# Turning six of the eight layer norm outputs by VectorE blocks and a DRAM round trip instead of TensorE transposes

## The chip, the cores and the metric

The kernel runs on one core of one Trainium2 chip. The metric is the device time of one execution in microseconds (us), the median of several runs; before the change it is 817.98 us (three runs, 817.22 to 819.26). The engines are named as the profile names them: PE is TensorE (matmuls) and PEld its weight loads, DVE is VectorE, ACT is ScalarE, POOL is GpSimd, SP is SyncE, on whose queue nearly all DMAs are issued.

## What is computed

One transformer block with adaptive layer norm, in float32, on x of 4 batches x 512 tokens x 256 features. Cut to what matters:

```
mod = silu(c) @ wmod                      # per batch: sa, ca, ga, sb, cb, gb
h = layernorm(x) * (1 + ca) + sa
x = x + ga * attention(h)                 # 16 heads of 128, causal
h = layernorm(x) * (1 + cb) + sb
x = x + gb * ffn(h)                       # router, 8 experts (2 chosen), shared, core
```

There are thus eight layer norms: one ahead of the attention and one ahead of the FFN, for each of four batches. Every matmul that follows contracts over the 256 features, so the normed tokens must be turned: from tokens on partitions to features on partitions.

## The kernel before, in words

**Precision.** A float32 matmul is made of three in a faster format (`mm3`, L138 to L142): each operand is kept as a rounded high part and a low part, the rest. The rest is a subtraction (`rest`, L147, L148). So L140, L141 and L142 stand for nearly all matmuls, and L148 for nearly all subtractions.

**The norm.** `normed` (L348) takes statistics and writes `xn`, 128 tokens on partitions, four token tiles t and two feature chunks c. `modulated` (L378) turns it: per chunk four TensorE transposes (L390) into a PSUM tile `ptn` of the tag "pj", which has three buffers and is shared with the projections; then scale and shift (on VectorE L397 for the first chunk, on ScalarE L395 for the second), ScalarE's copy of the high part `hTh` (L401) and VectorE's rest `hTl` (L148). The generator yields after each chunk, so that the second chunk's transposes come later in TensorE's order (`end_norm`).

**The attention.** The main loop (L1028) takes heads in groups of four per batch, and in each step scores one head, projects the next (`project`, L448), mixes an earlier one and projects out a still earlier one. A score tile (`ps`, two PSUM buffers) goes through VectorE's reduction (L488), ScalarE's exponential (L498), VectorE's reciprocal (L502) and GpSimd's scaling (L503). The weights `e` are turned too, but not on TensorE: `turned` (L506) has VectorE turn 32x32 blocks (L512, L518) into `T`, writes `T` to DRAM by four DMAs (L524) that set the blocks in place, and loads the result `aT` by one (L528). `parted` (L531) splits `aT` on ScalarE (L535) and GpSimd (L148), and `mixed` (L540) multiplies it by the values, two to three steps later.

**The FFN.** `all_ffn` (L928) runs the chunks of the experts over one batch after another. It begins while the last heads are still mixed. `route` (L599) makes the gates of a batch by a chain of small VectorE and ScalarE instructions (L621 to L676), and writes them to DRAM; `first` (L780) loads an expert's gates into a tile of the tag "spread" (L788, two buffers). `expert` (L846) adds up on VectorE and GpSimd (L859, L863).

**Order.** Only TensorE's order is the program's; the other engines and the DMA queue are put in order when the kernel is built, by a scheduler that estimates times. [...] The norms stand in it so:
- Attention norms: `norm_batch` of batch b + 1 with the first head of batch b's first group, `modulate` two heads later. The very first is made before the loop.
- FFN norms: `finish` (L1001) puts `norm_batch` one step after the last head of a batch is projected out, and `modulate` two steps after that for batches 0 and 1, three for batch 2, and six for batch 3. `route` follows one step later.

Of the kernel before, what the change touches and what calls it, by code (L numbers as in the profile page):

```python
# [11 lines left out]
F32 = mybir.dt.float32  # L12
F32R = mybir.dt.float32r
AF = mybir.ActivationFunctionType
ALU = mybir.AluOpType
# [3 lines left out]
P = 128  # L19
B, S, D = 4, 512, 256  # L20
H, DH = 16, 128
NT = S // P
DC = D // P
# [61 lines left out]
R = 32  # L85
NB = P // R
# [27 lines left out]
def adaln_attention_moe_kernel(  # L114
# [14 lines left out]
    nc = tc.nc  # L129
    const = ctx.enter_context(tc.tile_pool(name="const", bufs=1))  # L130
    work = ctx.enter_context(tc.tile_pool(name="work", bufs=2))
    small = ctx.enter_context(tc.tile_pool(name="small", bufs=2))
    psum = ctx.enter_context(tc.tile_pool(name="psum", bufs=2, space=PSUM))
    dram = ctx.enter_context(tc.tile_pool(name="dram", bufs=1, space=bass.MemoryType.DRAM))
# [9 lines left out]
    def f32(a: bass.AP) -> bass.AP:  # L144
        return a.bitcast(F32)

    def rest(eng, lo, full, hi):  # L147
        return eng.tensor_tensor(lo, full, f32(hi), ALU.subtract)  # L148
# [150 lines left out]
    modT = const.tile([P, 8, B], F32, tag="modT", name="modT")  # L299
# [48 lines left out]
    def normed(b: int, which: int):  # L348

        st = small.tile([P, NT, 6], F32, tag="st", name=f"st_{b}_{which}")  # L350
        mv = small.tile([P, NT, 2], F32, tag="mv", name=f"mv_{b}_{which}")
        for t in range(NT):
            nc.vector.bn_stats(st[:, t, :], xs[b][:, t, :])
        for t in range(NT):
            nc.vector.bn_aggr(mv[:, t, :], st[:, t, :])
        rstd = small.tile([P, NT], F32, tag="rstd", name=f"rstd_{b}_{which}")
        nc.gpsimd.tensor_scalar(rstd, mv[:, :, 1], LN_EPS, 1.0, ALU.add, ALU.mult)
        nc.gpsimd.tensor_tensor(rstd, rstd, minus_half, ALU.pow)
        xn = work.tile([P, DC, NT, P], F32, tag="xn", name=f"xn_{b}_{which}", bufs=1)
        for t in range(NT):  # L360
            nc.vector.tensor_scalar(
                xn[:, :, t, :],
                xs[b][:, t, :].rearrange("p (c d) -> p c d", c=DC),
                mv[:, t, 0:1],
                rstd[:, t : t + 1],
                ALU.subtract,
                ALU.mult,
            )
        return xn


    recent: dict[str, mybir.Instruction] = {}
# [5 lines left out]
    def modulated(b: int, which: int):  # L378


        xn = xns[b, which]
        hi = const.tile([P, DC, S], F32R, tag=f"hTh{b}", name=f"hTh_{b}_{which}")
        lo = const.tile([P, DC, S], F32R, tag=f"hTl{b}", name=f"hTl_{b}_{which}")
        (h2T if which else hT)[b] = hi, lo
        first = not (b or which)
        whole = []
        for c in range(DC):
            ptr = psum.tile([P, S], F32, tag="pj", name=f"ptn_{b}_{which}_{c}", bufs=3)
            for t in range(NT):
                nc.tensor.transpose(ptr[:, ts(t, P)], xn[:, c, t, :], ident)  # L390
            scale = modT[:, 4 * which + 2 + c, b : b + 1]
            shift = modT[:, 4 * which + c, b : b + 1]

            if c and not first:
                nc.scalar.activation(ptr, ptr, AF.Identity, bias=shift, scale=scale)  # L395
            else:
                nc.vector.tensor_scalar(ptr, ptr, scale, shift, ALU.mult, ALU.add)  # L397
            whole.append(ptr)

            for d in (c,) if not first else range(DC) if c == DC - 1 else ():  # L400
                nc.scalar.copy(hi[:, d, :], whole[d])  # L401
                recent["norm"] = rest(nc.vector, lo[:, d, :], whole[d], hi[:, d, :]).ins
            yield
# [5 lines left out]
    def norm_batch(b: int, which: int):  # L409
        if which and b > 1:  # L410
            with tc.issue_after(recent["hidden"]):
                xns[b, which] = normed(b, which)
            return
        xns[b, which] = normed(b, which)
# [563 lines left out]
    with tc.manual_schedule(engines={mybir.EngineType.DVE, mybir.EngineType.Activation}):  # L978
        for _ in modulated(0, 0):
            pass  # L980
# [9 lines left out]
    def modulate(b: int, which: int):  # L990

        m = modulated(b, which)
        next(m)
        begun_norms.append(m)
# [17 lines left out]
    b, h = order[0]  # L1012
# [15 lines left out]
    for n, (b, h) in enumerate(order):  # L1028
# [30 lines left out]
        e, _, exp, by_sum = next(scores)  # L1059
# [138 lines left out]
```

## Time and profile before

| | |
|---|---|
| median of three runs | 817.98 us |
| profiled execution, its own time | 815.89 us |
| span of the profiled execution | 814.1 us |
| mean granted TensorE clock | 0.989 |
| attention, some norms beside it | to about 640 us |
| FFN | from about 630 us |
| DMA traffic | 124.12 MB, 152 GB/s in the mean |

The span reaches from the first to the last instruction of the program; what lies around it is 815.89 - 814.1 = 1.8 us. Groups of instructions are listed by line, engine, operation and tile names (output<-inputs), with a count, a duration and what ended the idle time before them. A duration is that of one instruction from start to end; matmuls overlap, so the price of one in a full stream is read from the distance of starts. The norms that the change touches have their transposes at 79 and 85 us (attention, batch 2), 119 and 123 (attention, batch 3), 569 and 573 (FFN, batch 0), 608 and 613 (batch 1), 653 and 656 (batch 2) and 701 to 702 us (batch 3).

### The profile page before, as it was taken

What the parts mean: (1) busy time and instruction counts of PE and PEld (TensorE: products, weight loads), DVE (VectorE), ACT (ScalarE), POOL (GpSimd) and SP (SyncE); (2) the same over time, 40 slices, a digit from 0 to 9 for tenths busy, and PEclk for the clock granted to TensorE, in tenths of its full rate; (3) what the DMA queues carried; (4) which work ended last, traced back from release to release, by engine and by line L of the source; (5) the groups of instructions that cost most, each with busy time, mean ns of one, the idle gap of its engine ahead of it and who ended that gap; (6) DMA issues with size and microseconds to landing.
All of it is one profiled execution on the core that took longest, in us unless ns stands there. A gap on an engine that the chain in (4) does not pass through costs nothing.

```text
span 814.1 us, 14111 instructions
## 1 busy us (share of the span) xinstructions
PE 776.6 (95%) x4487; PEld 671.2 (82%) x4487; DVE 596.6 (73%) x1734; ACT 490.1 (60%) x1184; POOL 520.6 (64%) x523
## 2 busy tenths in 40 slices
PE   6898999999999999999999999999998998989997
PEld 5677898999978999998899999999887766767775
DVE  5976888777657777766777677778898587795555
ACT  3575667666656765665666666666656334656663
POOL 4665566896756688675656886656556245565675
PEclk9999999999999999999999999999999899999999
DMA  7376454665775456657555675644576333322221
GB/s 234 102 254 190 130 156 132 183 184 155 219 229 158 135 171 186 179 159 209 160 145 159 174 194 146 186 132 140 153 195 206 105 123 85 101 57 74 57 82 61
DMA packets 73218, 124.12 MB, mean 152 GB/s; under 512 B 8996, under 2 KB 51252, under 8 KB 73144
## 3 DMA queue, kind: packets, MB, share of 16 engines
q1 hardware_dynamic: 73112, 123.21, 52.4%
q8 instruction: 36, 0.59, 0.3%
q14 instruction: 38, 0.31, 0.1%
q0 software_dynamic: 32, 0.02, 0.0%
HBM read 73.05 MB, written 50.14 MB: 151 GB/s over the span
## 4 chain that ended last, share of the span: by engine, by line
PE 72%; DVE 10%; DMA 7%; POOL 4%; ACT 2%; issue 2%; SPq 2%; DVEq 0%; ACTq 0%; POOLq 0%
PE acc L835 4%; PE ps L140 3%; PE pz L140 3%; PE pz L141 3%; PE pz L142 3%; PE ps L141 3%; PE ps L142 3%; PE po L140 3%; PE po L141 3%; PE po L142 3%; PE pk L141 3%; PE pk L140 3%; PE pk L142 3%; PE pv L140 3%; PE pv L142 3%; PE pv L141 3%
## 5 line engine op out<-in xcount | busy, mean ns | idle before, releaser
L148 POOL TENSOR_TENSOR aT<-aT,aTh 128x1152 fp32r<-128x1152 f32 x64 | 172.0, 2687 | 109.0 <-ACT aTh L535 105.9
L503 POOL TENSOR_SCALAR e<-e,inv 128x128 f32<-128x128 f32 (+3 forms) x256 | 135.1, 542 | 68.7 <-DVE inv L502 66.2
L498 ACT ACTIVATE e<-e,nmax 128x128 f32<-128x128 f32 (+3 forms) x256 | 143.3, 561 | 49.7 <-DVE nmax L488 48.9
L535 ACT CAST aTh<-aT 128x1152 fp32r<-128x1152 f32 x64 | 74.0, 1157 | 122.8 <-DMA aT<-moved 61.9
L488 DVE CUSTOM_DVE_ANT_0 e<-ps,mask 128x128 f32<-128x128 f32 (+3 forms) x256 | 120.3, 478 | 28.6 <-PE ps L482 17.8
L518 DVE STREAM_TRANSPOSE T<-e 128x384 f32<-128x384 f32 (+2 forms) x256 | 100.5, 445 | 10.2 <-POOL e L503 10.1
L140 PE MATMUL ps<-kh,ql 128*128 128x256 f32 (+2 forms) x192 | 71.6, 373 | 12.4 <-DVE nmax L488 12.4
L148 DVE TENSOR_TENSOR zl<-pz,zh 128x512 fp32r<-128x512 f32 x64 | 43.9, 687 | 48.9 <-ACT zh L553 48.2
L140 PE MATMUL po<-wo,zl 128*128 128x256 f32 x256 | 73.1, 286 | 1.0 <-DVE zl L148 1.0
L140 PE MATMUL pv<-wv,hTl 128*128 128x256 f32 x256 | 72.0, 281 | 0.5 <-DVE hTl L148 0.5
L141 PE MATMUL po<-wo,zh 128*128 128x256 f32 x256 | 72.1, 282 | 0.0
L142 PE MATMUL po<-wo,zh 128*128 128x256 f32 x256 | 72.0, 281 | 0.0
L141 PE MATMUL pv<-wv,hTh 128*128 128x256 f32 x256 | 71.5, 279 | 0.0
L142 PE MATMUL pv<-wv,hTh 128*128 128x256 f32 x256 | 71.5, 279 | 0.0
L502 DVE RECIPROCAL inv<-tot 128x1 f32<-128x1 f32 x256 | 40.2, 158 | 40.8 <-ACT e L498 33.6
L863 POOL TENSOR_TENSOR oacc<-oacc,part 128x512 f32<-128x512 f32 x28 | 40.9, 1461 | 43.4 <-DVE part L859 36.5
L141 PE MATMUL ps<-kl,qh 128*128 128x256 f32 (+2 forms) x192 | 65.4, 340 | 0.3 <-DVE kl L148 0.3
L140 PE MATMUL pz<-aTh,vl 128*128 128x512 f32 (+2 forms) x192 | 65.0, 339 | 0.0
L141 PE MATMUL pz<-aT,vh 128*128 128x512 f32 (+2 forms) x192 | 64.9, 338 | 0.0
L142 PE MATMUL ps<-kh,qh 128*128 128x256 f32 (+2 forms) x192 | 64.9, 338 | 0.0
L142 PE MATMUL pz<-aTh,vh 128*128 128x512 f32 (+2 forms) x192 | 64.9, 338 | 0.0
L140 PEld LDWEIGHTS ps<-kh,ql 128*128 128x128 f32 x192 | 36.5, 190 | 22.3 <-DVE nmax L488 15.3
(216 smaller groups left out, 2332.1 us busy)
## 6 DMA issues: line engine op xcount, KB each, us to landing
moved<-T SPq DMA_DIRECT2D x256, 160.0 KB, 2.8
aT<-moved SPq DMA_DIRECT2D x64, 640.0 KB, 4.0
spread<-gates_e SPq DMA_DIRECT2D x32, 256.0 KB, 3.3
st_wqk<-in_wqk SPq DMA_DIRECT2D x16, 256.0 KB, 3.7
wf_first<-wfp_first SPq DMA_DIRECT2D x5, 512.0 KB, 4.7
st_wv<-in_wv SPq DMA_DIRECT2D x8, 256.0 KB, 3.3
st_wo<-in_wo SPq DMA_DIRECT2D x8, 256.0 KB, 3.4
wmod<-in_wmod SPq DMA_DIRECT2D x6, 256.0 KB, 5.6
```

The lines of the kernel that those rows point to most:

```text
L140: nc.tensor.matmul(o, lhsT=wl, rhs=mh, start=start, stop=False)
L141: nc.tensor.matmul(o, lhsT=wh, rhs=ml, start=False, stop=False)
L142: nc.tensor.matmul(o, lhsT=wh, rhs=mh, start=False, stop=stop)
L148: return eng.tensor_tensor(lo, full, f32(hi), ALU.subtract)
L488: least = nc.vector.tensor_tensor_reduce(out=et, in0=ps[:, :n], in1=maskf[:, S - n :], scale=-SCALE, scalar=BIG, op0=ALU.add, op1=ALU.min, ...
L498: exp = nc.scalar.activation(et, et, AF.Exp, bias=nm[:, t : t + 1], scale=-1.0, accum_out=tot[:, t : t + 1])
L502: nc.vector.reciprocal(inv[:, one], tot[:, one])
L503: by_sum = nc.gpsimd.tensor_scalar(et, et, inv[:, one], 1.0, ALU.mult, ALU.mult)
L518: nc.vector.transpose(to[:, first : first + n], blocks[:, at : at + (n - 1) * step + 1 : step])
L535: nc.scalar.copy(hi, full)
L835: nc.tensor.matmul(acc, lhsT=w2(k, b), rhs=act[:, s], start=c == 0, stop=c == n - 1)
L863: recent["added"] = nc.gpsimd.tensor_tensor(oacc, oacc, to, ALU.add).ins
```

## The change

The outputs of the first two attention norms are still turned by TensorE (`by_pe`). For the six others, `normed` itself has VectorE turn each chunk in 32x32 blocks into a tile `ntb`, of the tag "spread" for the first chunk and "tmp" for the second; four DMAs a chunk write it to DRAM (`nm`), and one DMA a chunk loads it back with features on partitions, into `hF` (`nhf` in the trace), which takes over the one buffer of the tag "xn". `modulated` then has no TensorE work: ScalarE writes the high part by scale and shift from `hF`, VectorE applies the same scale and shift in place and takes the rest. Both read and write SBUF. All of it, other than TensorE's transposes before, is put in place by the scheduler.

```diff
@@ normed @@
-        return xn
+        return xn if by_pe(b, which) else moved_norm(b, which, xn)
+
+    def by_pe(b: int, which: int) -> bool:
+        return which == 0 and b < 2
+
+    def moved_norm(b: int, which: int, xn):
+        moveds = []
+        for c in range(DC):
+            tag = ("spread", "tmp")[c]
+            tb = work.tile([P, NB, NT * R], F32, tag=tag, name=f"ntb_{b}_{which}_{c}")
+            nc.vector.transpose(
+                tb.rearrange("p i (t r) -> p t i r", r=R),
+                xn[:, c].rearrange("p t (i s) -> p t i s", s=R),
+            )
+            moved = dram.tile([NB, R, NB, NT * R], F32, tag=f"nmoved{c}", name=f"nm_{b}_{which}_{c}")
+            for a in range(NB):
+                nc.sync.dma_start(
+                    moved[:, :, a, :].rearrange("i s x -> s i x"), tb[a * R : (a + 1) * R]
+                )
+            moveds.append(moved)
+        hF = work.tile([P, DC, NB, NT, R], F32, tag="xn", name=f"nhf_{b}_{which}", bufs=1)
+        for c, moved in enumerate(moveds):
+            nc.sync.dma_start(
+                hF[:, c].rearrange("p a t r -> p a (t r)"),
+                moved.rearrange("i s a x -> (i s) a x"),
+            )
+        return hF
@@ modulated @@
         (h2T if which else hT)[b] = hi, lo
+        if not by_pe(b, which):
+            by_block = "p (t a r) -> p a t r"
+            for c in range(DC):
+                full = xn[:, c]
+                scale = modT[:, 4 * which + 2 + c, b : b + 1]
+                shift = modT[:, 4 * which + c, b : b + 1]
+                hi_c, lo_c = (a[:, c, :].rearrange(by_block, a=NB, r=R) for a in (hi, lo))
+                nc.scalar.activation(hi_c, full, AF.Identity, bias=shift, scale=scale)
+                nc.vector.tensor_scalar(full, full, scale, shift, ALU.mult, ALU.add)
+                recent["norm"] = rest(nc.vector, lo_c, full, hi_c).ins
+                yield
+            return
         first = not (b or which)
```

## The prediction, before the changed kernel was run

> **What bounds the kernel now.** I read the page first (busy shares and slices), then the windows, the tile that the change removes, the order of work on TensorE and VectorE where the norms stand, the chain of waits, and the DMA queue.
>
> ```profile
> span 814.1 us, 14111 instructions
> PE 776.6 (95%) x4487; PEld 671.2 (82%) x4487; DVE 596.6 (73%) x1734; ACT 490.1 (60%) x1184; POOL 520.6 (64%) x523
> ```
>
> ```profile
> 130.00:140.00 10.00, 10.00 (x63) 9.07 (x62) 8.07 (x26) 6.63 (x19) 7.37 (x8) 1.00 0.44 125
> ...
> 630.00:640.00 10.00, 8.99 (x37) 7.34 (x37) 9.33 (x31) 3.22 (x6) 3.73 (x3) 0.68 0.32 74
> ...
> 670.00:680.00 10.00, 7.90 (x24) 5.02 (x25) 9.97 (x23) 3.70 (x9) 6.59 (x8) 0.83 0.22 56
> ```
>
> Columns of a window: length, then busy us of PE, PEld, DVE, ACT, POOL, then the granted TensorE clock. From 90 to 590 us TensorE is the bound: no idle time in nearly every window, so a microsecond of its work taken away shortens the span. From 590 to 680 it is not: TensorE idles, VectorE is busy 9.3 to 10 of 10, and after two of the gaps the clock falls (0.68, 0.83). The transposes that go are these:
>
> ```profile
> L390 PE MATMUL ptn<-ident,xn x64: 270/273/477, 10.3 to 702.2; 128*128 128x128 f32 x64
> L401 ACT CAST hTh<-ptn x16: 564/588/607, 12.7 to 704.2; 128x512 fp32r<-128x512 f32 x16
> L148 DVE TENSOR_TENSOR hTl<-ptn,hTh x16: 651/690/692, 13.5 to 704.9; 128x512 fp32r<-128x512 f32 x16
> L397 DVE TENSOR_SCALAR ptn<-ptn,modT x9: 789/817/819, 11.9 to 702.2; 128x512 f32<-128x512 f32 x9
> L395 ACT ACTIVATE ptn<-ptn,modT x7: 750/762/767, 45.6 to 702.5; 128x512 f32<-128x512 f32 x7
> ```
>
> 273 ns is the time of one, not its price, since matmuls overlap. The price is read from starts on TensorE:
>
> ```profile
> 122.77 0.40 PE L142 MATMUL pk<-hTh,wqk 128*128 128x512 f32 x1
> 123.14 0.63 PE L390 MATMUL ptn<-ident,xn 128*128 128x128 f32 x4
> 123.53 0.48 PE L140 MATMUL ps<-kh,ql 128*128 128x512 f32 x1
> 123.84 0.39 PE L141 MATMUL ps<-kl,qh 128*128 128x512 f32 x1
> ```
>
> Undisturbed, starts are 0.23 apart, so L141 would start at 123.23; it starts at 123.84, which makes 0.61 for a group of four. Other groups, by the same sum: 0.45 at 119.25, 0.67 at 85.3, 0.59 at 572.6, and 1.05 for the eight at 701.4. I take 1.07 per norm batch.
>
> [...] The kernel already does this for its attention weights, whose rows price it below. [...] L641 takes 260 ns alone, but
>
> ```profile
> 629.88 2.64 POOL L148 TENSOR_TENSOR aT<-aT,aTh 128x1152 fp32r<-128x1152 f32 x1 [1.65 <-ACT aTh L535]
> ```
>
> ```profile
> 631.18 1.49 DVE L641 TENSOR_TENSOR lt<-lt,r_f 32x128 f32<-32x128 f32 x1
> ```
>
> it ends only after that GpSimd instruction. The change moves hTl's two inputs (one was in PSUM) into SBUF. [...]
>
> **Part by part**, for six of eight batches: attention norms 2 and 3, FFN norms 0 to 3; I call them A2, A3, F0 to F3.
>
> TensorE loses 6 x 1.07 = 6.4 us. A2, A3, F0, F2 and F3 (701 us) lie where it is the bound: -5.3. F1's (608 to 613) stand just ahead of waits on VectorE, so it would only wait longer: 0. No PSUM tile is taken (ptn shares "pj" with projections); that I cost at nothing, from 0 to -0.4 a batch (F2's transposes waited for it some 0.4).
>
> VectorE gains two 128x512 block transposes. The rows for T<-e are 268, 405 and 553 ns for 128, 256 and 384 columns; continued, 0.70 each, 1.40 a batch (bounds 1.1, twice the 0.55 of 384 columns, to 1.5). Both chunks get tensor_scalar on SBUF instead of one in PSUM: L361 took 391 ns at its least for 256 columns, so 0.53 to 0.69 for 512; 2 x 0.66 - 0.82 = +0.5. GpSimd waits: the like instruction al<-hid,ah has a mean of 1016 ns against 671 alone, xn 589 against 391, so 2 x 0.35 + 2 x 0.2 = +1.1 (0 to 4, four waits of less than half a 2.69 us aT). In all 3.0 us a batch. ScalarE: two activations of 0.76 write the high parts directly: 1.5 in place of 0.76 + 2 x 0.59, so -0.4.
>
> SP's queue gets ten more DMAs a batch. Four moved<-T take 1.86 to issue, an aT 0.34, so 8 x 0.465 + 2 x 0.34 = 4.4. More matters that each load hF waits at the head of the queue for its four writes:
>
> ```profile
> SPq L528 <- DMA moved<-T: 123.0, 129, 3.1
> ```
>
> ```profile
> moved<-T SPq DMA_DIRECT2D x256, 160.0 KB, 2.8
> aT<-moved SPq DMA_DIRECT2D x64, 640.0 KB, 4.0
> ```
>
> In the built program's order the pieces of that head's moved stand among and behind these loads, and its aT behind them all. From blocks done, 3.7 for eight writes, 2.6 to land, 3.5 for a load: about 9.8 us to the second half, and aT some 5 to 6 us later than now. GpSimd finishes aT 12 us before TensorE takes it (107.7 against 95.1 for one head), so pz itself isn't late. But aTh and the new activation stand in ScalarE's fixed order ahead of the q and k copies of the next head, and kl is ready only 3.45 us before use (heads of 96 to 200 us, from kl's end to its matmul). The nearest rows are the heads that prepare FFN weights, with two to five extra DMAs, loads and ScalarE waits: eight such units cost TensorE 1.19 + 1.55 in the windows 230 to 250 and 0.94 + 0.66 + 0.57 in those of 370 to 410, 4.9 us or 0.6 each. So A2, A3, F0: 3 x 0.6 = +1.8 (0 to 3.4 each). The block transposes come 10 us and 20 VectorE instructions before the modulation; VectorE has 2 us free a head.
>
> F1 falls into the last attention heads, and here the chain of waits runs through the very transfer that is delayed:
>
> ```profile
> 603.55 3.08 DMA moved<-T
> 606.71 6.60 DMA aT<-moved
> ...
> 617.62 0.69 DVE hTl L148
> ```
>
> From there it goes by e, zl, aT and again zl to TensorE at 633.3. F1's blocks now precede that head's T; nm, hF, a weight load and the gates precede its aT: blocks 600.7, writes issued by 604.4, landed 607, other moved pieces 608, aT issued 610.5, not 606.7: +3.8. Against this the norm's own ptn, hTh and hTl, 1.8 on that chain, come earlier: +2.0 (-1 to +5).
>
> F2's blocks fall at 638 on a busy VectorE, and push zl: +0.3; its modulation finds VectorE idle (2.08 busy in 640 to 650): 0. F3's blocks (1.4) now stand between the steps of batch 2's routing. VectorE is busy without a break from 663.4 to 685, and TensorE waits 2.93 at 673.8 for an activation queued behind a routing one: +1.4, and 0.6 [...]: +2.0 (0.5 to 4). Its modulation moves from 702 to 680: 3.6 us idle at 685 absorb the rest. The tag "spread" is shared with the gate rows of the experts: the issue of one such load goes from 667 to about 676, it lands at 679, and its expert's sum, now at 677.1, wants it at 678.5: in that range.
>
> Sum: -5.3 + 1.8 + 2.0 + 0.3 + 2.0 = +0.8, with the profiled execution's own 815.89 making 816.7. The median of the three runs is 817.98, 2.1 above it, so I forecast 818.8.
>
> **Rivals.** First, the waits are hidden: scheduled order puts aTh later in ScalarE's queue, the 12 us of cover hold, F1 gains by its modulation. Then -6.4 + 0.3: 811.9. For it: TensorE is the bound in 95%, and ScalarE and VectorE have 40% and 27% free. Against it: SP's waits already reach ScalarE (61.9 us of aTh waiting for aT), and the windows at 590 to 680. Second, slower, one mechanism: F1's load trip. If hF's second half lands after about 611, VectorE's in-order modulation holds the score reductions that free TensorE's two score tiles, and ScalarE holds k's copies (kl's cover is 1.93 there, zl's 0.06): +5 by the chain, one more idle window at half clock [...], and F3 at the end of its range, 4: -5.3 + 1.8 + 5 + 1.7 + 0.3 + 4 = +7.5: 825.5. It decides when the trip from blocks to second half exceeds some 10 us, which is where my sum stands. For it: 6.60 for one load there, beside weight loads. Against: 1 MB a batch is little for queues half busy. Third, the stages before 590 gain and the later ones return exactly that; the built order shows that the transposes do go and the DMAs do come, so "it does nothing" is excluded.
>
> **How the numbers follow.** Measurement of this kernel can tell some 0.3%, 2.5 us: faster is below 815.5, slower above 820.4. Hidden waits 0.27 (810.5 to 815.4); sum as above, 0.45, own range 815.5 to 822.5, of which 0.32 within the bound and 0.12 above, 0.01 below; F1's trip 0.28 (822 to 829). Faster 0.28, same 0.32, slower 0.40. Range 811.5 to 826.5 leaves 0.1 on either side.
>
> **What would show it.** TensorE's rows for ptn 16 instead of 64; T's new rows 0.7 us; hTl's mean over 0.69; idle TensorE in the windows of A2, A3 and F0 under 1 us (else the cover was misjudged); aT at about 606 issued 4 us later relative to its T; TensorE's restart now at 633.3 later by 2; its wait at 673.8 longer by 1 to 2. A TensorE that starts its FFN run 5 us later or shows a new stretch of half clock makes the second rival right; one that starts it earlier, the first.

## The result and the profile after

The changed kernel takes 829.6 us in the median of four runs (826.33 to 830.82), the kernel before 817.63 beside it: a ratio of 1.0144, 95% interval 1.0120 to 1.0168, so 12 us slower where 1 was forecast. The profiled execution has a span of 824.6 us, 10.5 longer than before. The head of the page after:

```profile
span 824.6 us, 14135 instructions
PE 773.7 (94%) x4439; PEld 666.7 (81%) x4439; DVE 599.9 (73%) x1752; ACT 489.2 (59%) x1178; POOL 523.7 (64%) x523
```

The 48 transposes are gone (4487 to 4439 matmuls), TensorE has 2.9 us less to do, VectorE 3.3 more, and the program is 10.5 us longer: work does not explain it, waiting does. Windows of the profile after, with the columns of the prediction's windows:

```profile
100.00:110.00 10.00, 8.55 (x52) 7.41 (x52) 8.56 (x31) 5.28 (x15) 7.71 (x8) 1.00 0.62 179
110.00:120.00 10.00, 7.39 (x34) 6.14 (x33) 7.96 (x24) 4.93 (x13) 5.51 (x6) 0.83 0.34 81
...
130.00:140.00 10.00, 8.42 (x52) 7.29 (x51) 5.46 (x21) 7.96 (x21) 7.32 (x6) 1.00 0.48 139
...
580.00:590.00 10.00, 8.26 (x51) 6.92 (x50) 5.91 (x21) 6.84 (x17) 6.36 (x5) 1.00 0.46 143
```

Before, TensorE was busy 10.00 in every one of them. From 110 to 120 it lost time twice: 2.6 us of idling, and a halved clock for a part of the rest (0.50 from 116 to 118, 0.83 in the mean of the ten). The moved norm's rows after, by tile (duration of one, least, median and most, then first and last start):

```profile
L431 PE MATMUL ptn<-ident,xn x16: 272/375/454, 10.4 to 43.5; 128*128 128x128 f32 x16
...
L382 DVE STREAM_TRANSPOSE ntb<-xn x12: 656/670/693, 72.8 to 676.4; 128x512 f32<-128x512 f32 x12
...
L421 ACT ACTIVATE hTh<-nhf,modT x12: 797/818/822, 81.3 to 687.2; 128x512 fp32r<-128x512 f32 x12
L422 DVE TENSOR_SCALAR nhf<-nhf,modT x12: 508/546/635, 82.9 to 689.9; 128x512 f32<-128x512 f32 x12
L148 DVE TENSOR_TENSOR hTl<-nhf,hTh x12: 650/686/1652, 84.4 to 691.7; 128x512 fp32r<-128x512 f32 x12
```

So the added instructions cost what the prediction gave them (0.67 for a block transpose, 0.55, 0.82), and hTl did not grow: the median is 686 ns (690 before). One of twelve took 1.65 us (687.54 to 689.19), ending 0.55 us after two GpSimd subtractions (gxl, 685.62 to 688.64).

**Where the time came from.** The lag of the changed kernel, read from the start of each head's first pz matmul in both traces (heads counted 0 to 63; the times are those of the kernel before):

| stretch | lag at its start and end, us | change | prediction |
|---|---|---|---|
| to head 3 (89 us): A2's trip is issued, its transposes are gone | 0, -0.7 | -0.7 | in the next row |
| heads 3 to 9 (89 to 145): what follows from A2; A3 | -0.7, +6.1 | **+6.8** | -0.9 |
| heads 9 to 53 (to 557) | +6.1, +5.3 | -0.8 | 0 |
| heads 53 to 57 (to 597): F0 | +5.3, +9.6 | **+4.3** | -0.5 |
| heads 57 to 63 (to 648): F1 | +9.6, +9.0 | -0.6 | +2.0 |
| to the end: F2, F3 | +9.0, +10.5 | +1.4 | +0.2 |

The loss is made at three norms within the attention (A2, A3, F0), where TensorE is the bound, not at the transition. A lag from one trace is rough: in runs that leave A2 as it was (e8, e11, e12, e17, e18) it is -1.5 to +1.4 at head 3. TensorE's idle times there, from its order of work after:

```profile
103.16 0.44 PE L140 MATMUL ps<-kh,ql 128*128 128x384 f32 x1 [1.45 <-DVE nmax L529]
...
115.21 0.69 PE L140 MATMUL ps<-kh,ql 128*128 128x384 f32 x1 [2.61 <-DVE nmax L529]
...
588.30 0.44 PE L140 MATMUL ps<-kh,ql 128*128 128x384 f32 x1 [1.74 <-DVE nmax L529]
```

Two more stand at 136.92 (1.58 us) and 599.57 (1.83; 0.96 before, and the clock is 0.84 in the ten us after it). All wait for VectorE's score reduction (nmax), which frees one of two score tiles. Why was that late? Followed back at A2: the order of SP's queue, before and then after.

```profile
73.59 1.88 SPq L524 DMA_DIRECT2D moved<-T  x4
78.03 0.34 SPq L528 DMA_DIRECT2D aT<-moved  x1
```

```profile
72.93 0.80 SPq L565 DMA_DIRECT2D moved<-T  x2
73.77 3.94 SPq L388 DMA_DIRECT2D nm<-ntb  x8
77.88 0.34 SPq L394 DMA_DIRECT2D nhf<-nm  x1
78.26 1.73 SPq L565 DMA_DIRECT2D moved<-T  x1
80.87 0.34 SPq L394 DMA_DIRECT2D nhf<-nm  x1
81.25 1.78 SPq L565 DMA_DIRECT2D moved<-T  x2
84.15 0.34 SPq L569 DMA_DIRECT2D aT<-moved  x1
```

A head's four writes of T are split in two by eight writes (3.94 us to issue), two loads and their waits; the last `moved` piece ahead of aT even belongs to the next head. aT is issued 6.1 us later; A3's is 9.6 us later (124.78 against 115.21), of which TensorE's own lag there is 4 to 5. ScalarE and VectorE after, at A2:

```profile
88.93 1.16 ACT L576 CAST aTh<-aT 128x1152 fp32r<-128x1152 f32 x1 [2.18 <-DMA aT<-moved]
89.99 0.71 ACT L539 ACTIVATE e<-e,nmax 128x512 f32<-128x512 f32 x1
```

```profile
90.83 0.16 DVE L543 RECIPROCAL inv<-tot 128x1 f32<-128x1 f32 x1 [2.49 <-ACT e L539]
```

ScalarE stands 2.18 us for aT with an exponential behind it, whose score reduction had ended at 87.67; VectorE stands 2.49 us for that exponential with all its later work behind it. Before, ScalarE stood for this aT as well:

```profile
82.03 1.16 ACT L535 CAST aTh<-aT 128x1152 fp32r<-128x1152 f32 x1 [2.66 <-DMA aT<-moved]
```

But VectorE stood there for 1.32 us at most, so what counts is when aTh comes and what then stands behind it. A head later VectorE is still behind: from 96 to 107 us its score reductions start 1.6 to 2.3 us later than before (96.07 against 93.79 for one), while TensorE's lag is still -0.7 to +1.0. At A3 VectorE's order holds the new work as well:

```profile
110.03 1.95 DVE L361 TENSOR_SCALAR xn<-x,mv,rstd 128x256 f32<-128x256 f32 x4 [1.19 <-POOL rstd L358]
111.90 0.41 DVE L148 TENSOR_TENSOR vl<-pv,vh 128x256 fp32r<-128x256 f32 x1
112.23 1.35 DVE L559 STREAM_TRANSPOSE T<-e 128x384 f32<-128x384 f32 x3
113.51 1.26 DVE L382 STREAM_TRANSPOSE ntb<-xn 128x512 f32<-128x512 f32 x2
114.69 0.27 DVE L559 STREAM_TRANSPOSE T<-e 128x128 f32<-128x128 f32 x1
114.88 0.26 DVE L529 CUSTOM_DVE_ANT_0 e<-ps,mask 128x128 f32<-128x128 f32 x1
```

The score reduction of 114.88 is the one that TensorE awaits at 115.21.

### The profile page after: what moved, and what is told of

The parts are those of the page before. It is cut to its first block, busy times and chain, and to the rows that moved or that the text cites. A ratio compares the mean times of both kernels' runs of the same rounds, so it can differ in the third digit from the quotient of the medians.

```text
span 824.6 us, 14135 instructions
## 1 busy us (share of the span) xinstructions
PE 773.7 (94%) x4439; PEld 666.7 (81%) x4439; DVE 599.9 (73%) x1752; ACT 489.2 (59%) x1178; POOL 523.7 (64%) x523
```

## The experiments

Two theories. **Queue theory**: the trip's DMAs delay aT, aT holds ScalarE, ScalarE holds VectorE. **VectorE theory**: the added VectorE work, block transposes above all, stands ahead of the score reductions. The kernel before was timed beside each run, with medians of 816.6 to 817.3. Ratios have their 95% intervals. Single executions of one kernel differ by up to some 8 us from its median (814.92 and 822.52 in e17), so a lag from one trace is read at one stage, and the verdict is the ratio's. The edits are shown shortened. The runs that leave out the trip or the blocks, and e4, do not turn the norm and so compute something else; they serve for their times alone.

### Where: attention norms or FFN norms

```diff
     def by_pe(b: int, which: int) -> bool:
-        return which == 0 and b < 2
+        return which == 1 or b < 2      # e1: attention norms only
+        return which == 0               # e8: FFN norms only
```

> Only the attention norms of batches 2 and 3 are moved; the four FFN norms are turned by TensorE as before. Every theory that puts the loss where the traces lag most (98 to 142 us, +6.8, after a gain of 0.7) expects about 6 us over the kernel before, 823 to 824. If the whole loss were at the transition and in the FFN (the prediction's F1 and F3), it would be 815.5 to 817.5.

> Only the four FFN norms are moved, the attention norms stay on TensorE. If the parts add up: the kernel before 817.3, plus 829.6 less the 826.0 of attention norms only, so 820.9. If the FFN norms lose only because they inherit a VectorE that is late, or gain once undisturbed, 815 to 818; if the transition alone can cost what the prediction's second rival had, 824 or more.

e1: 826.0 us, ratio 1.0109 (1.0087 to 1.0132). e8: 820.44, ratio 1.0026 (1.0010 to 1.0041). The parts add up: 8.7 and 3.2 us of 12. Three quarters of the loss come from two attention norms, for which the prediction had a gain of 0.9.

### Which part of SP's order

e2 puts the writes of T behind the aT of the head before (`issue_after` the aT load). e3 gives out the two loads of hF after that head's aT. e4 lets the loads read another array, so that they wait for no write.

```diff
+        recent["aT"] = nc.sync.dma_start(aT, moved.rearrange("i s a x -> (i s) a x")).ins
...
+        order.enter_context(tc.issue_after(recent["aT"]))   # e2: ahead of the writes of T
...
+        with tc.issue_after(recent["aT"]):          # e3: the two loads, after turned()
...
-                moved.rearrange("i s a x -> (i s) a x"),
+                wqk[c],                             # e4
```

> All six norms moved; the one edit keeps a head's load aT ahead of the next head's writes in SP's queue. In the changed kernel one write of the next head stands ahead of aT at both attention norms and waits for that head's T. Queue theory, form 1 (this inversion holds aT, aT holds ScalarE and GpSimd): the loss at 98 to 142 us falls from 6.8 to 2 or less, 823 to 826 in all. VectorE theory (two block transposes and longer modulations stand ahead of the score reductions): nothing changes, 828.5 to 830.5. Queue theory, form 2 (the loads' waits for their writes do it alone): nothing changes either.

> All six norms moved; the two loads of hF are issued only after the aT of that head, so that no load's wait and no other head's write stands ahead of aT; the eight writes stay where they were. Queue theory, either form: the attention norms lose 1 or less, F0 and F1 about 1.5 each less than now: 818 to 822. VectorE theory: 828 to 831.

> All six norms moved, all DMAs issued, but the two loads of hF read a piece of an input of the same shape in place of what was written, so that they don't wait for the eight writes (the normed values are left out of the result). One write of the next head still stands ahead of aT in SP's queue. Queue theory, form 1 (inversion): 827 to 830 as now. Form 2 (waits at the head of the queue): 819 to 824. VectorE theory: 828 to 830.

| | time | ratio | aT issued at A2 (before: 78.0) | lag at head 9 |
|---|---|---|---|---|
| after | 829.6 | 1.0144 (1.0120 to 1.0168) | 84.2 | +6.1 |
| e2, other head's write behind aT | 825.49 | 1.0115 (1.0089 to 1.0140) | 84.8 | +6.1 |
| e4, loads don't wait | 824.3 | 1.0098 (1.0077 to 1.0119) | 82.6 | +6.5 |
| e3, both, by loads behind aT | 823.3 | 1.0080 (1.0053 to 1.0108) | 81.1 | +2.1 |

Both single forms of the queue theory fail at the attention norms: with the inversion gone, or with the wait gone, aT is still 4.6 to 6.8 us late and the lag the same. With both gone it falls by 4, of which 2 may be scatter: at head 3 the three runs stand at -2.3, -2.8 and -2.7, the changed kernel at -0.7, so from there to head 9 e2 loses 8.4, e4 9.3, e3 4.8 and the changed kernel 6.8. The waits of 1.45 and 2.61 us at 103 and 115 us are not in e3's trace, though every VectorE instruction is (one of 1.38 stays at 132.9); in their place TensorE waits 0.73 and 0.89 us at 90 to 92 us for hTl, since hF now comes later. So the block transposes are not enough by themselves for those two waits. That e2 and e4 are 4 to 5 us faster than the changed kernel in their medians is not made at the attention norms: e2's interval overlaps the changed kernel's, and e4's lag falls from +7.7 at head 57 to +5.2 at the end.

### Trip or blocks: each left out

```diff
-            moved = dram.tile([NB, R, NB, NT * R], F32, tag=f"nmoved{c}")   # e5, e9, e11
...
-        return hF
+        return by_block(xn)                         # the modulation reads xn
...
-            nc.vector.transpose(                    # e6, e12, e16
-                tb.rearrange("p i (t r) -> p t i r", r=R),
-                xn[:, c].rearrange("p t (i s) -> p t i s", s=R),
-            )
```

> All six norms: VectorE's block transposes, scale, shift and rest stay, ScalarE's activation stays, but the eight writes and two loads are left out, and the modulation reads the norm's own tile instead (so the turning itself is left out of the result). VectorE theory (the block transposes stand ahead of the score reductions that free TensorE's score tiles, which is how VectorE is ordered here too): most of the loss at 98 to 142 us stays, 4 to 6 of 6.8, 823 to 827 in all. Queue theory (the trip delays aT): the loss at 98 to 142 goes, 814 to 818.

> All six norms: the writes, the loads and their waits stay, and only VectorE's two block transposes a batch are left out; the writes take the norm's own tile (so the turning is left out of the result). VectorE theory: the loss at 98 to 142 us falls to 1 or less, 817 to 821 in all. Queue theory: it stays at 5 or more, 826 to 830.

> Attention norms of batches 2 and 3 only, as in the run that gave 826.0, without their writes and loads (the modulation reads the norm's own tile; the turning is left out of the result). VectorE's block transposes stay. Queue theory (the trip delays aT, aT holds ScalarE's order, and that VectorE's): 815 to 818, at or below the kernel before, 817.2. VectorE theory: 822 or more.

> Attention norms only, as in the run that gave 826.0, without VectorE's block transposes but with the whole trip (turning left out of the result). This closes the square of trip and blocks: both 826.0, no trip 817.3. Queue theory alone: 823 to 826. If it takes both, the trip's delay and the blocks ahead of the score reductions, to use up the slack: 816 to 819.

| | all six norms | attention norms only |
|---|---|---|
| trip and blocks | 829.6, 1.0144 (1.0120 to 1.0168) | 826.0, 1.0109 (1.0087 to 1.0132) |
| blocks, no trip | 818.5, 1.0010 (0.9994 to 1.0025) | 817.34, 1.0005 (0.9994 to 1.0016) |
| trip, no blocks | 821.67, 1.0039 (1.0022 to 1.0057) | 818.43, 1.0017 (1.0003 to 1.0031) |

Neither theory alone holds at the attention norms. By the queue theory e16 should have kept its 6 to 9 us, by the VectorE theory e9 should have. Each half by itself costs the attention norms 1.6 us or less, both together 8.7. Both halves save TensorE's 2.1 us, which may hide a part of their cost; with it the halves cost 2.1 and 3.7, which makes 3.7 for both when the saving is taken off once, against 8.7 measured. Leaving the blocks out also changed SP's order, so aT has to be looked at: in e16 it is late as well (issued at 82.7, though ahead of the next head's writes), with a like stall of VectorE, in its order of work:

```profile
89.17 0.69 DVE L148 TENSOR_TENSOR kl<-pk,kh 128x512 fp32r<-128x512 f32 x1 [2.29 <-ACT kh L504]
```

but TensorE's order shows only one wait of over 1 us from 76 to 146 us,

```profile
94.32 0.44 PE L140 MATMUL ps<-kh,ql 128*128 128x384 f32 x1 [1.61 <-DVE nmax L525]
```

and none from 100 to 130 us, where the changed kernel has 1.45 and 2.61. In e9, with aT on time (77.7), TensorE waits 0.89 and 1.32 us at 111 and 122 us, where VectorE's reductions are up to 3.0 us later than before, and makes that up: its lag at head 9 is +0.2. This suggests a joint theory: two score tiles give VectorE a certain slack; the stall uses a part of it, the new work another, and only the sum runs over it. That the two halves cost far more together than apart is shown for the attention norms by the square above. That the slack of the score tiles is the reason is a reading of the traces; its size is not measured, and the order of the other work was not the same in the four runs. Nor does the square part the two effects of the trip, an aT that is late and a modulation that waits for hF. The second alone isn't enough: ScalarE waits for hF in e16 too (1.77 and 1.21 us; 1.51 and 1.06 in the changed kernel).

### The blocks one head later, and everything moved out of aT's way

e7 gives out the attention norms' blocks, writes and loads one head later, after its first score reductions. e10 and e14 are complete versions of the attention norms alone: e10 takes the norm one head earlier and the loads behind aT; e14 has xn one head earlier, the blocks behind score reductions, and all ten DMAs behind aT. e15 adds F0 and F1 in e14's manner.

```diff
+            if h == 1 and not by_pe(b + 1, 0):      # e7; normed() returns xn
+                with tc.issue_after(least):
+                    xns[b + 1, 0] = moved_norm(b + 1, 0, xns[b + 1, 0])
...
-            if h == 0:                              # e10, e14
+            if h == HG - 1 and b + 2 < B:
                 with tc.issue_after(least):
-                    norm_batch(b + 1, 0)
+                    norm_batch(b + 2, 0)
```

> All six norms; at the two attention norms the block transposes, writes and loads are given out one head later than the norm's xn, after that head's first score reductions. At batch 3's norm VectorE then has the block transposes behind the first two score reductions, not ahead of them; at batch 2's they stay behind the T of the head, as in the changed kernel. VectorE theory: the wait of 2.6 us with its half clock goes, 3 to 4 us less: 825 to 827. Queue theory: the loads come later still, 829 to 833.

> Attention norms only, complete, with nothing left out: the norm is given out one head earlier, so that the trip has a head more, and the two loads are issued behind the aT of that head. Block transposes, writes, loads and modulation are all there. Queue theory: aT is late by the eight writes only, and hF is there long before use: 815 to 819, against 826.0. VectorE theory (the block transposes cost where VectorE is busy; that head has the projection's sums on VectorE besides): 821 to 826.

> Attention norms of batches 2 and 3 only, complete: xn one head earlier, the block transposes behind the next head's first score reductions, and all ten DMAs of the trip behind that head's aT in SP's queue; modulation where it was. All added work is there. Queue theory with VectorE's bursts taken out of the way: the two norms' 2.1 us of TensorE are gained, 814 to 817. If the added work costs wherever it stands: 819 to 824, as with the loads alone moved (820.1).

> As the run before, and the FFN norms of batches 0 and 1 in the same manner (blocks one head later behind score reductions, trip behind aT, modulation and routing one head later); batches 2 and 3 of the FFN by TensorE. Queue theory: 813 to 817. If VectorE's added work costs at the transition to the FFN, where it is busy all the time: 818 to 822.

e7, with nothing left out: 821.89, ratio 1.0062 (1.0045 to 1.0079), so 4.7 us slower than the kernel before where the changed kernel is 12: 7 come back by order alone, more than either theory had. It doesn't tell the theories apart, since aT is on time as well (issued at 77.7 at A2). e10: 820.08, 1.0042 (1.0025 to 1.0059), against 826.0; TensorE waits 3.40 us for a score reduction at 103.7, where VectorE now has the blocks ahead of it in a head that sums up a projection. e14: 821.82, 1.0062 (1.0040 to 1.0084), and here the queue theory failed outright: aT is on time at A2 (77.4) and 5 us are still lost. The trace shows waits that go with it: VectorE stands 1.54 us at A2 and 2.31 at A3 for hTh, behind ScalarE that waits for hF, and TensorE idles 1.51 at 94.1 and 3.0 in four waits from 122 to 136. The wait for aT was traded for one for hF. e15: 824.3, 1.0079 (1.0051 to 1.0108). None of the four beats the kernel before.

### The trip's DMAs alone, beside the transposes

```diff
+        if which or b > 1:                          # in normed() of the kernel before
+            for c in range(DC):
+                ...
+                for a in range(NB):
+                    nc.sync.dma_start(moved[:, :, a, :], tb[a * R : (a + 1) * R])  # tb: of xn
+                nc.sync.dma_start(hF, moved)            # nothing reads this hF
         return xn
```

> The kernel before, complete, with the trip's DMAs alone added at the same six norms: eight writes of xn to DRAM and two loads of them into spare tiles that nothing reads. TensorE's transposes stay, VectorE and ScalarE get nothing to do. In SP's order half of a head's writes of T, and its aT, stand behind them, as in the changed kernel. Queue theory (aT issued late is enough): 4 to 10 us slower, 821 to 827, with TensorE waiting for score reductions at 95 to 120 us. VectorE theory, or one that needs both: 816.5 to 819.

838.21 us, ratio 1.0240 (1.0212 to 1.0268): 21 us slower, by DMAs that nobody waits for. At A3, ScalarE and then TensorE:

```profile
128.16 1.15 ACT L549 CAST aTh<-aT 128x1152 fp32r<-128x1152 f32 x1 [4.88 <-DMA aT<-moved]
129.21 0.26 ACT L480 COPY qf<-pq 128x128 f32<-128x128 f32 x1
```

```profile
130.50 1.12 PE L404 MATMUL ptn<-ident,xn 128*128 128x128 f32 x4 [4.56 <-DVE ql L148]
131.27 0.78 PE L140 MATMUL ps<-kh,ql 128*128 128x512 f32 x1
```

aT late holds ScalarE, q's copies stand behind aTh, q's PSUM tile stays taken, and TensorE's own transposes, which share that tag, wait for it. So a late aT can cost very different amounts: 1.6 us in e16, which has no such transposes, 10 at A2 and A3 here (lag at head 9: +10.0), and 5.5 each at heads 54 to 55 and 58 to 60 (F0, F1). The difference is read as what stands behind aT. VectorE got no work in this run. It shows that the trip's DMAs can be enough, where TensorE's transposes stand behind aT; in e16, where they don't, it takes the blocks too.

### The FFN norms

> FFN norms only, as in the run that gave 820.4, without their writes and loads (turning left out of the result). In the runs so far the lag that grows at 556 to 600 us stayed without DMAs (0.1 to 5.1) and nearly went without block transposes (3.4 to 4.2). If VectorE's added work is the cause at the FFN norms: 819 to 821. If the trip is: 814 to 817.5.

> FFN norms only, with writes, loads and their waits, without VectorE's block transposes (turning left out of the result). If VectorE's added work is the cause at the FFN norms: 815 to 818, against 820.4. If the trip is: 819.5 to 821.

e11: 819.9, ratio 1.0030 (1.0014 to 1.0046); e12: 824.56, 1.0077 (1.0043 to 1.0112), slower than with its blocks. Neither answer is clean, as the scheduler moved other work. Without blocks aT of F0's head is as late as with them (571.8 and 572.1 us; 564.5 before). Without DMAs the modulation came at once, into a GpSimd instruction; VectorE, then GpSimd in e11:

```profile
564.99 2.99 DVE L410 TENSOR_SCALAR xn<-xn,modT 128x512 f32<-128x512 f32 x2
```

```profile
564.57 2.67 POOL L148 TENSOR_TENSOR aT<-aT,aTh 128x1152 fp32r<-128x1152 f32 x1 [3.48 <-ACT aTh L564]
```

Two like those that take 0.55 each in the changed kernel need 2.99, the second ending 0.74 us after GpSimd does (567.24). That is the picture of the prediction's L641, 1.49 us beside aT instead of 0.26; why VectorE's end follows GpSimd's there is not shown. But late DMAs aren't needed for a loss at F0: in both runs without DMAs, e5 and e11, the lag grows by 4.3 over heads 53 to 57, as much as in the changed kernel, with F0's aT on time (issued at 567.6 in e11, with a lag of 3). Where e12's loss comes from stays open.

So the last two runs hold F0 alone fixed, and change only the place of its work: e17 as the change has it, e18 with blocks a head later, all DMAs behind aT, modulation and routing a head later.

```diff
+        return b > 0 or not which                   # by_pe, both
...
+                later.setdefault(n + 2, []).append((blocks, b))      # e18
-            later.setdefault(n + 3, []).append((modulate, b, 1))
+            later.setdefault(n + 4, []).append((modulate, b, 1))
```

> Only the FFN norm of batch 0 is moved, just as the change moves it: half of a head's writes and its aT stand behind the trip in SP's queue. aT 7 us late there, with the waits of ScalarE and VectorE behind it, as in the run of four FFN norms (lag +3 to +5 at heads 54 to 57, of which the kernel before has 1 by itself): 819 to 821. If a single norm is within the slack, as each half of the attention norms' change was: 816 to 817.5.

> The same norm alone, complete, with the trip behind aT in SP's queue, the block transposes one head later behind the first score reductions, modulation and routing one head later. All added work is there and 1.07 us of TensorE's is gone; in the run of four norms the lag at heads 54 to 57 shrank by 2.2. Queue theory: 814 to 816.5, at or below the kernel before. If the added work costs wherever it stands: 818 to 821.

e17: 822.52, ratio 1.0062 (1.0040 to 1.0083). e18: 818.49, 1.0029 (1.0017 to 1.0042). SP's queue in e17, then in e18:

```profile
559.60 0.78 SPq L565 DMA_DIRECT2D moved<-T  x2
560.47 4.07 SPq L388 DMA_DIRECT2D nm<-ntb  x8
...
570.30 0.34 SPq L569 DMA_DIRECT2D aT<-moved  x1
```

```profile
558.44 1.86 SPq L577 DMA_DIRECT2D moved<-T  x4
562.71 0.34 SPq L581 DMA_DIRECT2D aT<-moved  x1
...
572.06 4.06 SPq L396 DMA_DIRECT2D nm<-ntb  x8
```

From the first write of T to aT 10.7 us in one, 4.3 in the other. TensorE's longest wait in that stretch is 1.99 us in e17 and 0.81 in e18:

```profile
582.63 0.44 PE L140 MATMUL ps<-kh,ql 128*128 128x384 f32 x1 [1.99 <-DVE nmax L529]
```

Over heads 53 to 57 the lag grows by 3.7 in e17 and by 0.1 in e18, with the same work. So F0's loss, too, is one of place. Blocks, DMAs and modulation were moved at once; e5 and e11 say that it isn't the DMAs' place alone. e18 gains nothing for all that: it gives back 3.8 over heads 57 to 63, where the routing, one head later, lies among the next norm's work; that reading is from one trace. Nor is it settled why F0 alone costs more (1.0062) than the four FFN norms together (1.0026): in e17 the transposes of the next norm wait 3.15 us at 618.7 for q's rest, and in e8 there are none.

## Why the prediction was wrong, step by step

- **TensorE saves 1.07 a batch, 5.3 on the path.** Not shown. The transposes went, and busy time fell by 2.9, at a mean clock of 0.988 (0.989 before). No run has the saving without a cost, so it was not seen by itself.
- **VectorE: 3.0 a batch.** Mis-sized: 1.34 for the blocks and 2 x 0.55 - 0.82 = 0.28 for scale and shift, 1.6. The 1.1 of GpSimd waits did not come: median and least of hTl are unchanged (686 and 650 ns; 690 and 651 before). VectorE's busy time grew by 3.3 in all, not 18: the groups that the change touches by 10.7, while others, such as xn and steps of the routing, took 7.4 less.
- **SP's 4.4 us of issuing, aT 5 to 6 us late, pz not late.** Right: 3.94 + 2 x 0.34 = 4.6; aT 6.1 late at A2; and aT's rest still ends 4.9 us before pz at the worst head of A2 and A3.
- **"So A2, A3, F0: 3 x 0.6 = +1.8."** This is the step that failed. The path was named, aTh in ScalarE's fixed order ahead of k's copies, but priced from the heads that prepare FFN weights. Those heads have extra DMAs without putting aT back so far (4.9 to 6.0 us from the first write of T to aT, 4.3 in an undisturbed head, 11.2 at A2 after) and without new VectorE work ahead of the score reductions. By the lag the three norms cost 6.1 + 4.3 = 10.4 net, against -1.4 net in the sum. These 11.8 us cover the whole distance between forecast and result (829.6 - 818.8 = 10.8). The step took a small cost per late aT, to which VectorE's work would add nothing; what the runs show instead is that the late trip and the blocks together cost the attention norms 8.7 us, where each alone costs 0 to 1.6. F0's 4.3 is a matter of place too (e17, e18); which part of the work makes it stays open. "VectorE has 2 us free a head" was read from busy time, while by the joint theory the slack that counts is that of two score tiles.
- **F1: +2.0.** aT of its head is 13.5 us later in absolute time, 4 more than the lag of 9.5 there: the predicted 3.8. But in the sum over these heads nothing came of it, -0.6. Why is not settled.
- **F3: +2.0.** Right for the idle time: TensorE's 2.10 us at 673.8 (the prediction's 2.93 is the idle time of the weight load there) became 2.51 at 683.4 and 2.18 at 690.0, +2.6. The clock, 0.83 there before, stayed at 1.00, so less than that is left in the lag: +1.4 for F2 and F3 together, 0.2 in the sum. The 0.6 within the 2.0 was an estimate of the author's that no run shows by itself.
- **Rivals.** The first, hidden waits, falls with the 12 us; the third, gains before 590 that are returned later, with a lag of +5.3 already at 557. The second had the sign and, by 4 us, the time, but the wrong place: F1's load trip decided nothing, so its nearness is luck. Its kind of reasoning, a held ScalarE and VectorE in fixed order, belonged to A2 and A3. The prediction's own test, idle TensorE under 1 us in those windows "else the cover was misjudged", gave the answer at once: 1.45, 2.61 and 1.58 at A2 and A3, 1.74 at F0.

## What to carry to other kernels

Where DMAs are added to a queue that other transfers use, first list what stands behind each of them and who waits for that: here ten small DMAs put a load of another stage back by 6 us, and two engines stood in line behind it. Don't price such a delay by mean idle time: ask how far the engines may drift apart before the buffers between them (here, by our reading, two score tiles) stop one of them, and add up all that uses the same room, since two changes that each cost 1.6 us or less cost 8.7 together. When an experiment leaves work out under a scheduler, read its order of instructions before believing its time: in several runs here other work had moved with it.

## What the runs showed that was not expected

- Issuing alone took SP's queue long: eight writes of 64 KB took 3.9 to 4.1 us to issue at A2, A3 and F0, 0.5 each, and came between another transfer's four pieces, or ahead of them, for that long.
- DMAs that nobody waits for made the kernel 2.4% slower (e13).
- The length of a gap did not decide whether TensorE's clock was halved. After the gap of 2.61 us at 115.21 the matmuls started 0.43 us apart instead of 0.23 for some 3 us (clock 0.50 from 116 to 118, 0.83 from 110 to 120). At 70.55 the changed kernel had a gap of 2.49 us and the same effect (0.50 from 71 to 74, 0.83 from 70 to 80). The kernel before had 3.41 us at the same place, and the clock stayed at 1.00:

```profile
71.21 0.44 PE L140 MATMUL ps<-kh,ql 128*128 128x384 f32 x1 [3.41 <-DVE nmax L488]
71.49 0.33 PE L141 MATMUL ps<-kl,qh 128*128 128x384 f32 x1
71.66 0.34 PE L142 MATMUL ps<-kh,qh 128*128 128x384 f32 x1
```

  Ahead of the prediction's 0.68 and 0.83 the gaps were shorter as well (1.90 us at 629.81, 2.10 at 673.76; clock 0.50 from 630 to 636 and from 674 to 677). What does decide it is not shown. So executions of one kernel may differ by such stretches of half clock (the mean granted clock of e17's fourteen was 0.981 to 0.994): the one at 70.55 adds some 1.5 us to the lag. Ten us at 0.83 are 1.7 us of clock lost, which is what the second rival's sum has for one more such stretch.
